# A shared expert's second products, cut into two halves of the array

## The chip, the cores and the metric

The kernel runs on one core of a Trainium2 chip. The metric is the device time of one execution in microseconds (us), as the median of several runs. All data are float32. The engines are PE (matrix products; its weight loads have a row of their own, PEld), DVE (vector), ACT (activation), POOL and SP (which issue transfers, POOL also the indirect ones).

## The reference

The reference is one block of a network: gated cross attention, then a gated mixture of experts. `x` has 4 batches of 512 tokens of 512 features.

```python
x = x + tanh(g_xattn) * xattn(layernorm(x), ctx)      # 512 x 512 attention weights from ctx
n = layernorm(x)
shared = (silu(n @ Wg_s) * (n @ Wu_s)) @ Wd_s          # 512 -> 352 -> 512, for every token
probs  = sigmoid(n @ Wr + br + rb)                     # 8 experts, the best 2 per token
routed = sum over the 2 chosen e of w_e * (silu(n @ Wg[e]) * (n @ Wu[e])) @ Wd[e]
x = x + tanh(g_ffn) * (shared + routed)
```

The change lies in the last product of `shared`, the one with `Wd_s`.

## The kernel before, in words

The kernel works in three stretches of one program; loops are unrolled when it is built, and a tile framework places the waits and the order of each engine's queue.

The first stretch, up to about 181 us, computes the attention, the normalised rows, the routing and the shared expert's hidden values. For each of 16 tiles of 128 tokens, `shared_hidden` (L464) makes the products with `Wg_s` and `Wu_s`, `pg` and `pu`, 352 columns each, and sends the hidden rows through a scratch in memory, so that they come back in a layout that DVE can turn.

The second stretch is `shared_out`, about 181 to 235 us. For tile `n`, which this document calls group `n`, `shared_turned` has DVE turn the hidden values of the next tile (the stream transposes of L331) into `hT_s`, which has two buffers, each with three chunks (`NF` = 3) of 128 hidden values by 128 tokens. `shared_back` loads the hidden rows of a tile four ahead, and `shared_down` makes the second products. It calls `down` (L568): three products, accumulated in one PSUM tile `po`, each with a chunk of `hT_s` (128 x 128) as the weights that are held in the array, and 512 columns of `wsd` (which is `Wd_s`) streaming through. Then one DVE operation (L595) adds the scaled result to the tile of `x`, and a transfer on SP's queue (L596) stores it. `po` comes from the pool `ps_out`, which has two buffers.

Between the groups PE makes a few small products for the routing tables, each asked to come after the product before it: `pw` (L642, one column of weights, 39 columns streamed) before this stretch, and `pq` and `pi` (128 columns of weights, 39 streamed) behind groups 6 and 7. DVE makes the lists of rows from them, and POOL gathers the rows of the routed blocks with indirect transfers (L750).

The third stretch, up to about 499 us, is the loop over routed blocks: 128 gathered rows of one expert each, first products `rg` and `ru` (L785, eight of 352 columns) and second products `po` (L568 again, three of 512 columns), whose weighted results are added to the output by indirect transfers (L813). The last two groups of the shared expert, 14 and 15, are issued beside the first blocks. Block 0's rows are turned by DVE behind the update of group 13 (`after(turned, done, ...)`).

PE runs each product of the code as two passes, each with its own weight load and its own instruction, so the profile counts twice as many as the code. In the profile's rows `128*128` gives the rows and columns of the weights, and `128x512` the weights' depth and the columns that stream.

Of the kernel before, what the change touches and what calls it, by code (L numbers as in the profile page):

```python
# [9 lines left out]
F32 = mybir.dt.float32  # L10
# [7 lines left out]
P = 128  # L18
# [4 lines left out]
def flamingo_block(  # L23
# [16 lines left out]
    nc = tc.nc  # L40
    B, S, D = x.shape
# [9 lines left out]
    NF = len(FT)  # L51
# [21 lines left out]
    ps_out = ctx.enter_context(tc.tile_pool(name="ps_out", bufs=2, space=PSUM))  # L73
# [64 lines left out]
    def after(later, earlier, reason="written before it is read"):  # L138
        tc.add_manual_dep(
            later.ins, earlier.ins.name,  # L140
            mybir.DependencyInfo(mybir.DependencyClass.Sync, mybir.DependencyReason.DATA),
            reason=reason,
        )
# [22 lines left out]
    hT_s = [sp.take(NF, P) for _ in range(2)]  # L166
# [26 lines left out]
    wsd = const.tile([P, NF, D], F32, tag="wsd", name="wsd")  # L193
# [131 lines left out]
    def from_quarters(by, z, engine=nc.sync):  # L325

        return engine.dma_start(out=z, in_=by.rearrange("(p b) w -> p (b w)", b=NQ))
# [7 lines left out]
    product = {}  # L335
# [228 lines left out]
    def down(hT, wdj):  # L564

        po = ps_out.tile([P, D], F32, tag="out", name="po")
        for j in range(NF):
            product["last"] = nc.tensor.matmul(  # L568
                po, lhsT=hT[:, j, :], rhs=wdj(j), start=(j == 0), stop=(j == NF - 1)
            )  # L570
        return po

    def shared_back(n, behind=None):
        if n < B * NS:
            back = from_quarters(
                hs_d[n * NQ * P : (n + 1) * NQ * P, :],
                zhs_v[n % AHEAD].rearrange("p b w -> p (b w)"), nc.scalar,
            )
            if behind is not None:
                after(back, behind, "it comes in early enough")  # L580

    def back_early(behind):
        for k in range(AHEAD):
            shared_back(k, behind)
# [5 lines left out]

    def shared_down(n):

        po = down(hT_s[n % 2], lambda j: wsd[:, j, :])
        xs = x_sb[n // NS][:, n % NS, :]
        done = nc.vector.scalar_tensor_tensor(xs, po, tgf, xs, ALU.mult, ALU.add)  # L595
        nc.sync.dma_start(out=out[n * P : (n + 1) * P, :], in_=xs)  # L596
        return done

    def shared_out(b, lo=0, hi=NS, behind=None):
        for n in range(b * NS + lo, b * NS + hi):  # L600
            if n == 0:
                shared_turned(0, behind[0])
                shared_turned(1, behind[1])
            elif n + 1 < B * NS:
                shared_turned(n + 1)
            shared_back(n + AHEAD, product.get("out"))
            done = product["out"] = shared_down(n)
        return done
# [72 lines left out]
    def count():  # L681
# [19 lines left out]
        out=tab.rearrange("b p t -> b (p t)"), in_=slot_d.rearrange("(b p) t -> b (p t)", p=P)  # L701
# [159 lines left out]
    last = SURE - 1  # L861
# [84 lines left out]
```

## Time and profile before

| what | value |
| --- | --- |
| median of 5 runs | 516.13 us (515.26 to 517.04) |
| profiled execution: its own time | 514.88 us |
| profiled execution: span from first to last instruction | 511.9 us |
| mean granted TensorE clock | 0.99 |
| PE busy | 493.6 us, 96% of the span |
| PEld, DVE, ACT, POOL busy | 275.3, 232.9, 91.4, 265.0 us |
| second products of the shared expert (L568, `po<-wsd,wqk`) | 96 passes, 42.2 us busy |
| second products of the routed blocks (L568, `po<-wbig,x_all`) | 222 passes, 101.4 us busy |
| first products of the routed blocks (L785) | 592 passes, 223.6 us busy |

How to read it: the busy time of PE counts the time in which at least one product is in the array, and a product's own duration (592 ns for 512 columns) is longer than the distance to the next one, since products follow each other through the array. The time between the starts of two products is therefore the better measure of what one costs. The span leaves out some 3 us around the program.

### The profile page before, as it was taken

Reading aid. Unit: us, or ns where it says so; the run is one execution under the profiler, and the core shown is the slowest. Engines: PE = TensorE matmul, PEld = TensorE weight load, DVE = VectorE, ACT = ScalarE, POOL = GpSimd, SP = SyncE. Lnnn points to the kernel's source line nnn. Section 1 sums busy time; section 2 is a strip of 40 time slices with the busy share of each in tenths; the row PEclk is TensorE's granted clock in tenths of the full one; section 3 lists DMA queues with packets and bytes.
Section 4 is the critical chain, followed back from the end, with each engine's and each line's share of the span. In section 5 each row is a group of like instructions: output and inputs, shape, how many; then the busy total and the mean of one; then the engine's idle time right before and its main releaser. Section 6 shows DMA issues by size and latency. Waiting matters only on the chain. (4 is left out here: it accounts for less than half of the span.)

```text
span 511.9 us, 5436 instructions
## 1 busy us (share of the span) xinstructions
PE 493.6 (96%) x1507; PEld 275.3 (54%) x1507; DVE 232.9 (46%) x542; ACT 91.4 (18%) x163; POOL 265.0 (52%) x293
## 2 busy tenths in 40 slices
PE   8999999999999999999999999999999999999980
PEld 4444464465677644455555555555555555555540
DVE  1898965855864447543323332233232233233210
ACT  3354034112023000001111111111110211111110
POOL 3004230171265510555777777777477776767331
PEclk9999999999999999999999999999999999999996
DMA  6999993579996978624556655665455665656433
GB/s 207 395 370 363 334 360 119 164 175 174 355 203 103 250 185 284 205 88 143 118 125 128 133 119 125 135 126 119 112 115 117 125 134 107 139 118 136 76 41 41
DMA packets 67164, 87.86 MB, mean 172 GB/s; under 512 B 32992, under 2 KB 40032, under 8 KB 67136
## 3 DMA queue, kind: packets, MB, share of 16 engines
q1 hardware_dynamic: 43056, 55.08, 34.9%
q0 software_dynamic: 13184, 25.88, 25.9%
q10 hardware_dynamic: 10896, 6.56, 5.2%
q8 instruction: 14, 0.23, 0.2%
q14 instruction: 14, 0.11, 0.1%
HBM read 56.78 MB, written 30.70 MB: 171 GB/s over the span
## 5 line engine op out<-in xcount | busy, mean ns | idle before, releaser
L750 POOL DMA_INDIRECT x_all<-xz_d,idx x148 | 141.4, 956 | 85.9 <-issue 35.8
L331 DVE STREAM_TRANSPOSE x_all<-x_all 128x512 f32<-128x512 f32 (+1 forms) x71 | 69.8, 984 | 156.7 <-DMA x_all<-by 141.2
L785 PE MATMUL rg<-wbig,x_all 128*128 x296 | 111.9, 460 | 1.8 <-PE po L568 1.0
L785 PE MATMUL ru<-wbig,x_all 128*128 x296 | 111.7, 459 | 0.0
L568 PE MATMUL po<-wbig,x_all 128*128 x222 | 101.4, 592 | 0.7 <-DVE x_all L836 0.7
L785 PEld LDWEIGHTS rg<-wbig,x_all 128*128 128x128 f32 x296 | 55.9, 190 | 43.3 <-issue 20.2
L813 POOL DMA_INDIRECT out_x<-ws,idx x37 | 59.6, 1611 | 29.4 <-issue 24.9
L785 PEld LDWEIGHTS ru<-wbig,x_all 128*128 128x128 f32 x296 | 56.2, 190 | 31.3
L568 PEld LDWEIGHTS po<-wbig,x_all 128*128 128x128 f32 x222 | 42.1, 190 | 44.0 <-issue 36.3
L398 PE MATMUL po<-wbig 128*128 128x512 f32 x128 | 56.4, 592 | 0.0
L464 PE MATMUL pg<-ws,wbig 128*128 128x352 f32 x128 | 49.3, 467 | 0.1
L464 PE MATMUL pu<-ws,wbig 128*128 128x360 f32 (+1 forms) x128 | 48.8, 462 | 0.0
L793 ACT ACTIVATE h_all<-rg 128x352 f32<-128x352 f32 x37 | 17.2, 464 | 173.2 <-issue 75.6
L317 POOL TENSOR_TENSOR rstd<-ve,mhalf 128x4 f32<-128x4 f32 x8 | 8.2, 1023 | 71.6 <-DVE ve L315 38.2
L812 ACT ACTIVATE ws<-po,wts 128x512 f32<-128x512 f32 x37 | 25.4, 687 | 103.1 <-PE po L568 47.5
L568 PE MATMUL po<-wsd,wqk 128*128 128x512 f32 x96 | 42.2, 594 | 0.0
L552 POOL DMA_INDIRECT slot_d<-ent,posi x32 | 31.0, 969 | 17.6 <-issue 10.1
L398 PEld LDWEIGHTS po<-wbig 128*128 128x128 f32 x128 | 24.2, 190 | 29.4 <-issue 27.5
L464 PEld LDWEIGHTS pu<-ws,wbig 128*128 128x128 f32 x128 | 24.3, 190 | 13.6
L464 PEld LDWEIGHTS pg<-ws,wbig 128*128 128x128 f32 x128 | 23.5, 190 | 12.2 <-issue 0.5
L568 PEld LDWEIGHTS po<-wsd,wqk 128*128 128x128 f32 x96 | 18.0, 190 | 21.3 <-issue 19.8
L795 DVE TENSOR_TENSOR x_all<-h_all,ru 128x352 f32<-128x352 f32 x34 | 17.5, 515 | 17.8 <-ACT h_all L793 14.0
(135 smaller groups left out, 335.0 us busy)
## 6 DMA issues: line engine op xcount, KB each, us to landing
wbig<-in_Wgu SPq DMA_DIRECT2D x8, 1408.0 KB
by<-x_all SPq DMA_DIRECT2D x34, 192.0 KB
x_all<-by SPq DMA_DIRECT2D x34, 192.0 KB
wbig<-in_Wd SPq DMA_DIRECT2D x8, 768.0 KB
x_all<-in_x SPq DMA_DIRECT2D x4, 1024.0 KB
wbig<-in_xT SPq DMA_DIRECT2D x4, 1024.0 KB
xz_d<-wbig POOLq DMA_DIRECT2D x16, 256.0 KB
wbig<-xz_d SPq DMA_DIRECT2D x16, 256.0 KB
```

The costliest lines, as they stand in the source:

```text
L317: power = nc.gpsimd.tensor_tensor(rstd, ve, mhalf, ALU.pow)
L331: return nc.vector.transpose(dst.rearrange("p c (j b) -> p b c j", b=NQ), z.rearrange("p b (c i) -> p b c i", i=Q))
L398: product["last"] = nc.tensor.matmul(po, lhsT=xT_v[b % 2][:, c, ts(s, P)], rhs=attT_v[b % 2][:, c, :], start=(c == 0), stop=(c == NN - 1),)
L464: product["last"] = nc.tensor.matmul(dst, lhsT=xnT_v[b % 2][:, c, ts(s, P)], rhs=ws[:, c, at : at + n], start=(c == 0), stop=(c == ND - 1),)
L552: sc = nc.gpsimd.indirect_dma_start(out=slot_d, in_=what, out_offset=bass.IndirectOffsetOnAxis(ap=where, axis=0), in_offset=None,)
L568: product["last"] = nc.tensor.matmul(po, lhsT=hT[:, j, :], rhs=wdj(j), start=(j == 0), stop=(j == NF - 1))
L750: g = nc.gpsimd.indirect_dma_start(out=z[:, q, :], out_offset=None, in_=xz_d, in_offset=at(idx4[:, q, i : i + 1]),)
L785: nc.tensor.matmul(dst, lhsT=xgT[:, c, :], rhs=wbig[:, bass.ds(base[i] + (c * 2 * H + lo), H)], start=(c == 0), stop=(c == ND - 1),)
L793: silu = nc.scalar.activation(sg, pg, AF.Silu)
L795: nc.vector.tensor_mul(h[:, :H], sg, pu)
L812: nc.scalar.activation(y, po, AF.Copy, scale=wts[:, i : i + 1])
L813: nc.gpsimd.indirect_dma_start(out=out, in_=y, out_offset=at(idx[:, i : i + 1]), in_offset=None, compute_op=ALU.add)
```

## The change

The second products of the shared expert are made by a new function, `down2`. It splits the 128 columns of weights (128 tokens) into two times 64. The first half is placed in columns 0 to 63 of the array and its results go to partitions 0 to 63 of `po`; the second half is placed in columns 64 to 127 and its results go to partitions 64 to 127. For each of the three chunks both halves stream the same 512 columns of `wsd`. The routed blocks keep `down`.

```diff
+    def down2(hT, wdj):
+
+        po = ps_out.tile([P, D], F32, tag="out", name="po")
+        for j in range(NF):
+            for t in range(2):
+                product["last"] = nc.tensor.matmul(
+                    po[t * 64 : (t + 1) * 64, :], lhsT=hT[:, j, t * 64 : (t + 1) * 64], rhs=wdj(j),
+                    start=(j == 0), stop=(j == NF - 1), tile_position=(0, t * 64),
+                )
+        return po
+
     def shared_back(n, behind=None):
...
     def shared_down(n):
 
-        po = down(hT_s[n % 2], lambda j: wsd[:, j, :])
+        po = down2(hT_s[n % 2], lambda j: wsd[:, j, :])
         xs = x_sb[n // NS][:, n % NS, :]
         done = nc.vector.scalar_tensor_tensor(xs, po, tgf, xs, ALU.mult, ALU.add)
```

## The prediction

> **What bounds the kernel now.** I read the page's engine shares first, then its groups, then busy time by stage, then the timeline around the lines that the change touches. Page, engines and the two groups that are replaced (count, busy us, mean ns, idle before):
>
> ```profile
> PE 493.6 (96%) x1507; PEld 275.3 (54%) x1507; DVE 232.9 (46%) x542; ACT 91.4 (18%) x163; POOL 265.0 (52%) x293
> ...
> L568 PE MATMUL po<-wsd,wqk 128*128 128x512 f32 x96 | 42.2, 594 | 0.0
> ...
> L568 PEld LDWEIGHTS po<-wsd,wqk 128*128 128x128 f32 x96 | 18.0, 190 | 21.3 <-issue 19.8
> ```
>
> PE is busy 96% of the span, and the shared expert's second products never wait (idle 0.0). The 48 products of the code stand as 96: each float32 product runs as two passes, each with its own weight load. Busy time by stage (PE, PEld, DVE, ACT, POOL; clock, DMA):
>
> ```profile
> 181.50:234.70 53.20, 52.33 (x142) 25.58 (x141) 30.73 (x52) 1.39 (x3) 17.23 (x21) 1.00 0.63 192
> 234.70:498.64 263.94, 261.38 (x790) 148.77 (x789) 81.81 (x109) 40.66 (x71) 183.10 (x167) 1.00 0.56 118
> 498.64:511.90 13.26, 1.36 (x4) 0.29 (x2) 0.00 (x0) 0.69 (x1) 1.57 (x1) 0.63 0.30 40
> ```
>
> The products lie in the first stage. The second, the routed blocks, has PE busy for 261.38 of 263.94 us at full clock. So whatever the first stage gains or loses on PE moves the end by as much. Weight loads of the first stage:
>
> ```profile
> 182.38 0.19 PEld L568 LDWEIGHTS po<-wsd,wqk 128*128 128x128 f32 x1 [0.24 <-issue]
> 182.81 0.19 PEld L568 LDWEIGHTS po<-wsd,wqk 128*128 128x128 f32 x1 [0.24 <-issue]
> ...
> 189.68 0.19 PEld L568 LDWEIGHTS po<-wsd,wqk 128*128 128x128 f32 x1 [0.24 <-issue]
> ```
>
> From 182.38 to 189.68 are 17 passes, 0.429 us each for 512 columns: that is the price of a pass. A load starts every 0.43 us, when the pass before its own starts, and is hidden under it. Loads are no limit here, so halving their width saves nothing.
>
> **The change, part by part.** It removes 48 products of 128 columns of weights (96 passes, 41.2 us) and adds 96 of 64 columns (192 passes). Each still streams 512 columns. Bytes, DMAs, DVE's, ACT's, POOL's and SP's instructions stay, in the same order. On PE the order is t=0, t=1 within each j, and 39 half products stand between the second set of small products and routed block 0 where 20 whole ones stood; 3 and 6 follow blocks 0 and 1 where 1 and 3 did.
>
> *Do the halves overlap?* No two products share the array in this trace. The bounds are 0 us extra (each pass of one half beside one of the other) and one pass of 0.429 us for each of the 96 added. The two halves write other partitions and hold other weights; nothing in the order makes the one wait for the other. I take overlap and keep the other end as a rival.
>
> *Stagger.* PE takes A-first, A-second, B-first, B-second in order (A, B the halves). A-second must wait for A-first, and B-first stands behind it. So B runs one pass late: A-second beside B-first, then B-second beside the next step's A-first. That costs one pass of 0.429 us for each uninterrupted run. The runs: groups 0 to 6; group 7; groups 8 to 13 with half of 14; the rest of 14; group 15. Before block 0 something else ends last:
>
> ```profile
> 217.64 3.17 PE L568 MATMUL po<-wsd,wqk 128*128 128x512 f32 x7
> ...
> 219.13 0.75 DVE L595 SCALAR_TENSOR_TENSOR x_all<-po,tgf,x_all 128x512 f32<-128x512 f32 x1 [1.05 <-PE po L568]
> ...
> 219.80 0.88 DVE L331 STREAM_TRANSPOSE wqk<-h_all 128x384 f32<-128x384 f32 x1
> ...
> 220.50 2.21 DVE L331 STREAM_TRANSPOSE x_all<-x_all 128x512 f32<-128x512 f32 x2
> ...
> 221.68 0.83 PE L785 MATMUL rg<-wbig,x_all 128*128 x2 [0.87 <-issue]
> ```
>
> Of the seven passes from 217.64 on, the third is group 13's last and ends streaming at 218.93 (217.64 + 3 x 0.43). DVE's update, its turn and block 0's turn then let block 0 start 2.75 us later, whatever PE does in between. So group 13's delay counts in full, the half of group 14 before block 0 is free, and the 3 half products after it need 4 passes in a row where 2 stood. One pass each for three runs, two for the fourth, one for the fifth: 6 x 0.429 = 2.6 us. Bounds 0 and 2.6; I take 2.6.
>
> *Array reshaped.* The nearest row is `pw`, one column of weights, between full ones (PE, then PEld):
>
> ```profile
> 178.21 0.76 PE L464 MATMUL pu<-ws,wbig 128*128 128x352 f32 x2
> 178.89 0.23 PE L642 MATMUL pw<-pick,eoff 128*1 128x39 f32 x2
> 179.05 0.86 PE L464 MATMUL pg<-ws,wbig 128*128 128x352 f32 x2
> ```
> ```profile
> 178.89 0.09 PEld L642 LDWEIGHTS pw<-pick,eoff 128*1 128x1 f32 x2 [0.49 <-issue]
> 179.05 0.30 PEld L464 LDWEIGHTS pg<-ws,wbig 128*128 128x128 f32 x2
> 179.45 0.19 PEld L464 LDWEIGHTS pu<-ws,wbig 128*128 128x128 f32 x1
> ```
>
> A 352-column pass takes 0.295 us (0.429 x 352 / 512). `pu`'s second starts at 178.50 and streams until 178.80, but `pw`'s load starts at 178.89: 0.09 us of drain. The two passes of `pw`, 39 columns each, need 0.07 us, until 178.96; the next load starts at 179.05: again 0.09. It is exposed: `pg`'s first pass lasts from 179.05 to 179.45, 0.10 more than its streaming. Leaving the split shape costs 0.09 + 0.10 = 0.19, entering it 0.09 + 0.056 (an exposed load of 64 columns, below) = 0.15. Five entries and four exits (the exit before block 0 lies in the idle 0.87): 5 x 0.15 + 4 x 0.19 = 1.5 us. Bounds 0 and 9 x 0.19 = 1.7.
>
> *Exposed loads.* Where products are short, loads set the pace:
>
> ```profile
> 199.55 0.86 PEld L642 LDWEIGHTS pq<-pick,ws 128*128 128x128 f32 x7 [0.24 <-issue]
> ```
>
> Seven loads in 0.86 us, the last 0.19 long: (0.86 - 0.19) / 6 = 0.112 us each for 128 columns, so I estimate 0.056 for 64. Today each load starts with the pass before its own and not earlier. If that holds, B-first's load starts when A-second starts, and B-first cannot start for 0.056 us, though its half is free; the next A-first stands behind B-second likewise. Two exposed loads a step, on the path for 46.5 steps (42 before group 14, 1.5, and 3): 93 x 0.056 = 5.2 us. Bounds: 0, if the queue pulls loads past a waiting product, and 93 x 0.112 = 10.4, if a narrow load is no faster. I take 5.2, since the row shows no load ahead of the product before it.
>
> *Added waits.* From group 2 on (and at the routed blocks 0 and 1) the first product also waits for its own engine's group two back, whose PSUM tile it takes. That group is always over by then, so it waits for nothing. The second wait puts an entry on PE's sequencer, 12 in the phase, 51 ns each by the trace. It is hidden because the sequencer reaches block 0's first entry at 218.1, 2.5 us before PE's last pass ahead of that block ends (220.65); uncovered, 12 x 0.05 = 0.6 us. DVE turns group n+1's input by 1.75 us after group n-1 ends (218.93 to 220.68 above); PE needs it after 2.57 us today, after 2.14 with the stagger: still covered.
>
> Sum: 2.6 + 1.5 + 5.2 = **9.3 us**. The profiled execution took 514.88 us (span 511.9 and 3.0 around it), so it would be 524.2. The median of the five runs, 516.13, is 1.25 above (0.24%): **525.4 us**. Runs of one kernel spread over 515.26 to 517.04, so 0.2%, 1.0 us, is about what a measurement can tell from no change.
>
> Two rules of the Trainium skill bear on this; no number here rests on them. "TensorE: Matmul & The Clock Gate", Part 3 on packing small matmuls, says that products in different tiles of the array start some 4 ns apart: by that estimate stagger and loads shrink to 96 x 0.004 = 0.4 us, and with the 1.5 the time is 518.0. Its measurements were of tiles with one product each, and no run here shows it for two passes. The same section says that a load overlaps running products only where the row groups differ; both halves use all rows, so by it every load would be exposed, 186 x 0.056 = 10.4 us, and the time 530.6. The trace contradicts it for today's loads, which lie under products of the same rows. "TensorEngine Tiling (Array Packing)", Overview, promises a factor only where a dimension is 64 or less; here it is 128, cut in two, so at best two half products cost what one did. That is a rule against a gain.
>
> **The rivals.**
> 1. *Loads pulled ahead.* As forecast, but B-first's load passes the waiting A-second: 2.6 + 1.5 = 4.1 us, 520.2. For: that half's earlier pass is over, so nothing holds its weights. Against: no load in the trace runs ahead of the product before it.
> 2. *The halves do not overlap.* 192 passes in a row. 42 steps more by 0.858 are 36.0; the half of group 14 after block 0 is 6 passes instead of 2, 1.7; group 15, 12 instead of 6, 2.6; with 1.5 for the shapes 41.8 us: **557.9**. For: all products of this trace run one behind the other, and nothing shows two at once. Against: no shared weights or partitions.
> 3. *Shorter passes, faster.* Were a pass of 64 columns of weights quicker, 96 passes on the path would gain. From rival 1's 4.1 us it breaks even at 4.1 / 96 = 0.043 us less a pass (0.386), and at half a pass (0.214) it saves 20.6 and the stagger halves to 1.3: 498.3. Against: `pw` with one column of weights and `pq` with 128 both have products of 198 ns over 39 columns; width does not set the pass.
> 4. *Nothing to measure.* Both halves start together, loads hidden and reshaping mostly covered by the drain: under 1 us, 516 to 517. With the 1.5 in full it would be 517.6, already slower.
>
> **How the numbers follow.** Forecast 0.38 (about 523 to 531), rival 1 0.27 (518 to 522), rival 2 0.25 (553 to 570, since exposed loads can add to it), in between 0.02, rival 4 0.05, rival 3 0.03. So faster 0.03, same 0.05, slower 0.92. The range goes from 518, below rival 1, to 560, above rival 2's sum. It leaves out rivals 3 and 4 and some 0.1 of rival 2's upper tail.
>
> **What would show it.** Passes of `po<-wsd,wqk` with 64 columns, 192 of them. Forecast: loads of `t`=1 start with the preceding pass and a pair of passes takes 0.485 us, the phase (181.5 to block 2's start) grows by 9. Rival 1: pairs at 0.429. Rival 2: starts 0.43 apart throughout and PE busy in the phase near 95 us. Rival 3: passes under 0.39. I am wrong in mechanism if PE idles for its own semaphore, if entering the split shape costs more than 0.2 us, or if the routed blocks change.

## The result and the profile after

The changed kernel takes 518.64 us (median of 30 runs, 516.27 to 522.89) beside 515.21 for the kernel before (56 runs, 513.27 to 520.96): a ratio of 1.0061, 95% interval 1.0044 to 1.0079, which is 3.1 us more (2.3 to 4.1). It is slower, as forecast, but by a third of the forecast 9.3 us. Here and below medians are over all runs, while ratios compare only runs in the usual state and leave out those in a slower one, with a lower granted clock, so that a ratio is not the quotient of the two medians. The profiled execution took 517.37 us, its span 515.5.

From the page, engines and the two groups that took the place of the old ones (in a group's row: count, busy us, mean ns, idle before; the lines of the code behind the new function have moved by 11):

```profile
PE 494.7 (96%) x1603; PEld 270.4 (52%) x1603; DVE 234.1 (45%) x542; ACT 91.2 (18%) x163; POOL 265.0 (51%) x293
...
L578 PE MATMUL po<-wsd,wqk 128*64 128x512 f32 x192 | 43.3, 595 | 1.9 <-DVE wqk L331 1.9
...
L578 PEld LDWEIGHTS po<-wsd,wqk 128*64 128x64 f32 x192 | 13.9, 137 | 28.5 <-issue 27.6
```

Twice the passes (192 for 96) keep PE busy for 43.3 us where it was 42.2, and a pass lasts as long as before (595 ns for 594). So two passes lie side by side nearly all the time. New is an idle 1.9 us: PE waited once for DVE's turn of a group's input. Busy time by stage (PE, PEld, DVE, ACT, POOL; clock, DMA):

```profile
180.50:237.80 57.30, 54.53 (x237) 21.31 (x236) 31.41 (x51) 1.39 (x3) 17.91 (x21) 1.00 0.58 180
237.80:502.00 264.20, 261.80 (x791) 149.01 (x790) 81.86 (x108) 40.66 (x71) 182.29 (x167) 1.00 0.55 118
502.00:515.50 13.50, 1.11 (x3) 0.19 (x1) 0.00 (x0) 0.69 (x1) 1.71 (x2) 0.67 0.28 39
```

The difference lies in the stretch of the change, 57.30 us for 53.20; the routed blocks behind it take 264.20 for 263.94. By the starts of products in the two traces: this stretch begins 0.97 us earlier than before (a difference of the unedited first stretch), block 0 starts 2.69 us later after its beginning, block 2 a further 1.44 us later after block 0, and the rest is 0.39 longer: 3.55 us, the difference of the spans. The device times of these two executions, 517.37 and 514.88 us, are only 2.49 apart, since 3.0 us lay around the span before and 1.9 lie around it now.

How the halves run shows in the loads and in the length of the uninterrupted runs on PE (start, length, engine, how many passes):

```profile
180.55 0.20 PEld L578 LDWEIGHTS po<-wsd,wqk 128*64 128x64 f32 x4 [0.49 <-issue]
181.03 0.14 PEld L578 LDWEIGHTS po<-wsd,wqk 128*64 128x64 f32 x2 [0.29 <-issue]
181.46 0.14 PEld L578 LDWEIGHTS po<-wsd,wqk 128*64 128x64 f32 x2 [0.28 <-issue]
```
```profile
180.55 18.25 PE L578 MATMUL po<-wsd,wqk 128*64 128x512 f32 x84
198.72 1.08 PE L653 MATMUL pq<-pick,ws 128*128 128x39 f32 x8
199.74 2.80 PE L578 MATMUL po<-wsd,wqk 128*64 128x512 f32 x12
202.46 0.66 PE L653 MATMUL pi<-pick,ws 128*128 128x39 f32 x4
203.06 10.52 PE L578 MATMUL po<-wsd,wqk 128*64 128x512 f32 x48
215.47 7.05 PE L578 MATMUL po<-wsd,wqk 128*64 128x512 f32 x30 [1.89 <-DVE wqk L331]
223.40 0.83 PE L796 MATMUL rg<-wbig,x_all 128*128 x2 [0.88 <-issue]
...
228.30 1.93 PE L578 MATMUL po<-wsd,wqk 128*64 128x512 f32 x6
...
237.82 0.86 PE L796 MATMUL rg<-wbig,x_all 128*128 x2
```

The same places in the kernel before:

```profile
181.52 18.19 PE L568 MATMUL po<-wsd,wqk 128*128 128x512 f32 x42
...
221.68 0.83 PE L785 MATMUL rg<-wbig,x_all 128*128 x2 [0.87 <-issue]
...
226.49 1.02 PE L568 MATMUL po<-wsd,wqk 128*128 128x512 f32 x2
...
234.66 0.76 PE L785 MATMUL rg<-wbig,x_all 128*128 x2
```

Four loads stand at the start, two for each half (each half's second load is put in behind its first pass), and from then on two loads every 0.43 us, both under the passes before. The passes start in pairs: 181.028 and 181.035, 181.458 and 181.464, 181.887 and 181.893, so 6 to 7 ns within a pair and 0.429 us from pair to pair. The 84 passes of the first run take 18.25 us; the 42 whole ones took 18.19. There is no late half and no exposed load inside a run. The row at 228.30 is the exception: group 14's rest behind block 0 is three half products, six passes, and takes 1.93 us (A is the half in columns 0 to 63, B the other). Two of B's passes start beside A's, then B's other two follow alone: four steps where the kernel before had two.

The new wait, seen on DVE (updates L606 and turns L331):

```profile
208.48 0.75 DVE L606 SCALAR_TENSOR_TENSOR x_all<-po,tgf,x_all 128x512 f32<-128x512 f32 x1 [1.04 <-PE po L578]
209.14 0.87 DVE L331 STREAM_TRANSPOSE wqk<-h_all 128x384 f32<-128x384 f32 x1
213.81 0.75 DVE L606 SCALAR_TENSOR_TENSOR x_all<-po,tgf,x_all 128x512 f32<-128x512 f32 x1 [3.79 <-PE po L578]
214.47 0.84 DVE L331 STREAM_TRANSPOSE wqk<-h_all 128x384 f32<-128x384 f32 x1
```

In groups 0 to 9, 12 and 13 the update starts 0.63 to 0.64 us after the start of the group's last pass. Group 10's last pass started at 210.41, so its update was due at 211.05; it started at 213.81, since PE's signal is recorded at 213.78, 2.8 us late, though all passes were in time. The turn for group 12 stood behind that update, and PE waited for it.

### The profile page after: what moved, and what is told of

Its sections match the earlier page's. It is cut to its first block, busy times and chain, and to the rows that moved or that the text cites. A ratio compares the mean times of both kernels' runs of the same rounds, so it can differ in the third digit from the quotient of the medians.

```text
span 515.5 us, 5641 instructions
## 1 busy us (share of the span) xinstructions
PE 494.7 (96%) x1603; PEld 270.4 (52%) x1603; DVE 234.1 (45%) x542; ACT 91.2 (18%) x163; POOL 265.0 (51%) x293
## 5 line engine op out<-in xcount | busy, mean ns | idle before, releaser
L331 DVE STREAM_TRANSPOSE x_all<-x_all 128x512 f32<-128x512 f32 (+1 forms) x71 | 70.0, 987 | 153.2 <-DMA x_all<-by 139.2
L804 ACT ACTIVATE h_all<-rg 128x352 f32<-128x352 f32 x37 | 17.2, 464 | 182.0 <-PE rg L796 83.5
L578 PE MATMUL po<-wsd,wqk 128*64 128x512 f32 x192 | 43.3, 595 | 1.9 <-DVE wqk L331 1.9
L578 PEld LDWEIGHTS po<-wsd,wqk 128*64 128x64 f32 x192 | 13.9, 137 | 28.5 <-issue 27.6
```

The source lines that it names most:

```text
L331: return nc.vector.transpose(dst.rearrange("p c (j b) -> p b c j", b=NQ), z.rearrange("p b (c i) -> p b c i", i=Q))
L578: product["last"] = nc.tensor.matmul(po[t * 64 : (t + 1) * 64, :], lhsT=hT[:, j, t * 64 : (t + 1) * 64], rhs=wdj(j), start=(j == 0), stop= ...
L804: silu = nc.scalar.activation(sg, pg, AF.Silu)
```

## The experiments

The theory after the result: (1) the two halves overlap because they are two halves of the array; (2) a half is fed past the other's waiting product, so neither stagger nor loads cost anything in a run; (3) what remains is reshaping, 0.35 us for each way in and out, and the uneven cut of group 14. The rivals: the overlap or the order comes from something else; the time is the late signal's; a reshaping costs less or more. Each kernel was timed against the kernel before on the same chip. Those chips were slower (before 522.59, 523.93 and 521.7 in the three sets), so ratios are what is compared.

**The changed kernel again**, unedited.

> The changed kernel once more, unedited. Theory (the halves run beside each other as pairs 0.429 us apart, and the loss is 1.4 us for reshaping the array plus 0.86 us because the half of group 14 is cut at an odd number of half products): some 2.2 to 3.5 us over the kernel before, and in the profile the pairs again 0.429 apart, with the 1.9 us in which PE waited for DVE gone or elsewhere. Rival (that wait is a lasting cost of the split): the same wait of about 1.9 us in the same group 12.

523.38 us (12 runs), ratio 1.0035 (1.0001 to 1.0070), or 1.8 us more: under the expected 2.2 to 3.5, which lies within the interval (0.1 to 3.7). The trace repeats the structure: 42.06 us from the first split product to block 0 (42.85 in the first profile, 40.16 before) and 19.26 from there to the first second product of the routed blocks, the same 19.26 as in the first, 17.71 before. A late signal came again, now in group 11 and 1.7 us late, and cost PE 0.9 us.

**One half's chunks first, then the other's.**

```diff
-        for j in range(NF):
-            for t in range(2):
+        for t in range(2):
+            for j in range(NF):
```

> All three products of the first half, then all three of the second. Theory (each half takes its next product from the queue on its own, past waiting products of the other half): pairs stay 0.429 us apart as long as the queue looks 12 instructions ahead, and the time is that of the changed kernel plus at most 0.9 us, since group 14 then leaves 6 passes behind block 0 instead of 4. Rival (products start strictly in the order of the program and the pairs seen are an order that was built in): the first half's six passes run alone and the second half's mostly too, about 4 passes more for each group, 16 x 4 x 0.429 = 27 us over the changed kernel.

533.11 us (4 runs), ratio 1.0192 (1.0130 to 1.0253). The start of its stretch:

```profile
187.55 0.19 PEld L578 LDWEIGHTS po<-wsd,wqk 128*64 128x64 f32 x2 [0.49 <-issue]
187.55 4.99 PE L578 MATMUL po<-wsd,wqk 128*64 128x512 f32 x20
188.03 0.14 PEld L578 LDWEIGHTS po<-wsd,wqk 128*64 128x64 f32 x1 [0.29 <-issue]
188.46 0.19 PEld L578 LDWEIGHTS po<-wsd,wqk 128*64 128x64 f32 x3 [0.29 <-issue]
188.89 0.19 PEld L578 LDWEIGHTS po<-wsd,wqk 128*64 128x64 f32 x2 [0.23 <-issue]
```

A's passes start alone at 187.548 and 188.028. B's first load starts at 188.462 and its pass at 188.463, 6 ns after A's third pass, while A's fourth to sixth were still to come. (Which half a pass belongs to is read from the distance: two of one half never start closer than 0.429 us, as the kernel with both in one half shows below.) So B does pass work that waits, but not from any depth. When A's third pass (the first of its second product) had just started, two products of A stood ahead: the one in work and one waiting whole, together five loads and passes waiting. At A's second pass there were seven, and B did not start. Each run of the stretch thus begins with two passes of A alone and ends with two of B alone (12 passes of group 7 took 3.70 us where the changed kernel took 2.80). Both simple stories, in order and unlimited, fail here.

**Two chunks of a half at a time.** This separates the two readings of that trace: a half is fed past one whole waiting product, or hardly past anything.

```diff
-        for j in range(NF):
-            for t in range(2):
+        for j, t in ((0, 0), (1, 0), (0, 1), (1, 1), (2, 0), (2, 1)):
```

> The changed kernel with the six half products of a group in another order: chunks 0 and 1 of the first half, chunks 0 and 1 of the second, then chunk 2 of the first and of the second. Where A's first pass of a run starts, five instructions wait ahead of B's first load (the product of A's second pass, loads and products of A's third and fourth). Theory (each half takes work past about five waiting instructions, not past seven): B's first load and pass start within 0.02 us of A's first pass, pairs stay 0.43 us apart, a group every 2.58 us, and the second stretch up to block 0 lasts about 42 us as in the changed kernel (41 to 43.5, a wait for DVE of up to 3 us as there aside); time within 0.3% of the changed kernel, some 1.004 of the kernel before. Rival (a half is fed past one waiting product only): B's first pass starts one or more passes late at the start of each run, 0.43 to 0.86 us for each of five runs, so 2.1 to 4.3 us more than the changed kernel, and single passes of A show at the run's start.

522.04 us (10 runs), ratio 1.0034 (0.9992 to 1.0075), that of the repeat of the changed kernel. Its first group:

```profile
186.92 0.20 PEld L577 LDWEIGHTS po<-wsd,wqk 128*64 128x64 f32 x4 [2.49 <-DVE eoff_i L705]
186.92 2.80 PE L577 MATMUL po<-wsd,wqk 128*64 128x512 f32 x12 [1.93 <-DVE eoff_i L705]
187.40 0.15 PEld L577 LDWEIGHTS po<-wsd,wqk 128*64 128x64 f32 x2 [0.28 <-issue]
```

B starts 13 ns after A (186.919, 186.932), with two products of A ahead of it, and the 12 passes take 2.80 us as in the changed kernel. By the count used above six loads and passes of A were waiting, since A's second load starts only at 186.972. The theory holds from a second side, and the rival (one or more passes late) is out. The stretch up to block 0 took 41.67 us. No signal of PE came late here; group 0's update started 0.34 us late, since DVE was still in a turn. The cut of group 14 behind block 0 is more uneven (two whole products of B, then chunk 2 of both): six steps where the changed kernel has four and the kernel before two, and the time from block 0 to the first routed second product is 20.12, 0.86 or two passes more than 19.26.

**Both halves in one half of the array.** Columns 0 to 63 and partitions 0 to 63 serve both; the sums of the two halves fall together and only 64 rows of each tile of `x` are updated.

```diff
-                    po[t * 64 : (t + 1) * 64, :], ...
-                    start=(j == 0), stop=(j == NF - 1), tile_position=(0, t * 64),
+                    po[:64, :], ...
+                    start=(j == 0 and t == 0), stop=(j == NF - 1 and t == 1), tile_position=(0, 0),
```

> Both 64-column products of each step are placed in columns 0 to 63, so that they share one half of the array; the sums of both go to the same 64 partitions, and only those 64 rows of x are updated. Theory (it is the two halves that let products run together): no overlap, 192 passes 0.429 us apart, 40 to 43 us over the kernel before, about 557. Rival (narrow products overlap or run faster wherever they stand): as the changed kernel, about 518.

561.97 us (one run), 39 us over the kernel before on that chip. The group on PE, and the same first run of 84 passes:

```profile
L578 PE MATMUL po<-wsd,wqk 128*64 128x512 f32 x192 | 83.5, 593 | 0.0
```
```profile
182.65 36.26 PE L578 MATMUL po<-wsd,wqk 128*64 128x512 f32 x84
```

Busy 83.5 us where the changed kernel has 43.3, and 36.26 us for the 84 passes that took 18.25. So the overlap comes from the two halves and from nothing else in the change, and it is worth what rival 2 had priced: by the trace 76.77 us up to block 0 and 23.54 from there to the first routed second product, 42.4 more than 40.16 and 17.71.

**The last two groups whole.** Groups 14 and 15 use `down` again; group 13's exit is then the last.

```diff
-        po = down2(hT_s[n % 2], lambda j: wsd[:, j, :])
+        po = (down2 if n < 14 else down)(hT_s[n % 2], lambda j: wsd[:, j, :])
```

> Groups 14 and 15, which stand beside the first routed blocks, keep whole products; groups 0 to 13 are split. Theory: two entries and two exits of the split shape (0.69 us by the changed kernel's trace) and the odd cut (0.86) go, 1.55 us less than the changed kernel, some 0.7 to 1.5 us over the kernel before. Rival (the loss lies in the split groups themselves, their waits or doubled instructions): no more than 0.4 us less than the changed kernel.

521.84 us (12 runs), ratio 0.9992 (0.9962 to 1.0022). From block 0 to the first routed second product it takes 17.71 us, as before to the hundredth, where the changed kernel takes 19.26:

```profile
230.24 1.02 PE L568 MATMUL po<-wsd,wqk 128*128 128x512 f32 x2
...
235.83 2.74 PE L568 MATMUL po<-wsd,wqk 128*128 128x512 f32 x6
```

So 1.55 us of the change are spent on group 14's cut and on going in and out around blocks 0 and 1. The stretch up to block 0 remains longer, 41.22 for 40.16. The ratio's interval is too wide to price the rest: it lies below that of the changed kernel in the first result, but overlaps that of the repeat on this chip (1.0001 to 1.0070), so that the saving is shown by the trace and not by the time.

**One chunk of three whole**, so that each group goes out of the split shape and back in.

```diff
         for j in range(NF):
+            if j == 1:
+                product["last"] = nc.tensor.matmul(
+                    po, lhsT=hT[:, j, :], rhs=wdj(j), start=False, stop=False
+                )
+                continue
             for t in range(2):
```

> In every group the products of j=0 and j=2 are split and that of j=1 is whole, so that the array is reshaped 16 more times in and out. Theory (each in and out costs 0.10 of drain and 0.107 of exposed load on leaving, 0.094 and 0.051 on entering, 0.35 us, as the changed kernel's trace has it): 16 x 0.35 = 5.6 us over the changed kernel, 7 to 9 over the kernel before. Rival (only the drains cost, the loads are hidden): 16 x 0.19 = 3.0, 5 to 6 over the kernel before. Rival (reshaping is free and the loss is elsewhere): as the changed kernel, 2 to 3 over.

529.34 us (12 runs), ratio 1.0084 (1.0049 to 1.0118): 4.4 us more than before. The groups on PE:

```profile
194.59 1.94 PE L583 MATMUL po<-wsd,wqk 128*64 128x512 f32 x8
196.46 1.13 PE L578 MATMUL po<-wsd,wqk 128*128 128x512 f32 x2
197.51 1.94 PE L583 MATMUL po<-wsd,wqk 128*64 128x512 f32 x8
```

From 194.59 to 197.51 are 2.92 us for a group; six passes of 0.429 are 2.57. So 0.35 us go to each way out and in, the 0.15 and 0.19 of the prediction; the groups that neither wait nor are interrupted all take this 2.92 us. The time does not confirm it: the theory expected 7 to 9 us over the kernel before, and 4.4 (2.6 to 6.2) fits the rival in which only the drains cost, 5 to 6. Against that rival stands the trace, where the loads are exposed in each group; why the timed loss is smaller is open. The signal of group 10 came 1.5 us late here. The first group's update came 2.2 us late too, but behind a turn of DVE that began only at 188.69; PE's signal had been there in time, at 187.15.

**Four quarters of 32 columns.**

```diff
-            for t in range(2):
+            for t in range(4):
-                    po[t * 64 : (t + 1) * 64, :], ...  tile_position=(0, t * 64),
+                    po[t * 32 : (t + 1) * 32, :], ...  tile_position=(0, t * 32),
```

> Four products of 32 columns each, in the four quarters of the array. Theory (every tile takes its own work from a queue that looks some six waiting instructions ahead): four passes at once; the fourth quarter's load stands behind up to nine waiting instructions and comes late, so the sets are 0.43 to 0.50 us apart and the time is 2 to 9 us over the kernel before. Rival (only two products can stream at once): 0.86 us for each set, 40 us over.

532.95 us (4 runs), ratio 1.0176 (1.0130 to 1.0221). The group on PE and the waits:

```profile
L578 PE MATMUL po<-wsd,wqk 128*32 128x512 f32 x384 | 44.6, 594 | 2.8 <-DVE x_all L606 2.2 <-DVE wqk L331 0.6
```
```profile
PE pu L464 <- DVE place L526: 4.6, 1, 4.6
PE po L578 <- DVE x_all L606: 2.2, 1, 2.2
```

Four passes start at once (191.734, .741, .747, .754) and the next four 0.429 us later, so 384 passes keep PE busy 44.6 us: the overlap holds for four tiles as for two. The expected delay of the fourth quarter did not come. Its load for the next product starts at 191.755 with nine loads and passes waiting ahead of it, three of each other quarter; so the limit that the two kernels above had shown, six waiting but not seven, is not one on their sum. A limit for each tile would fit all these kernels, but was not tested by itself. The time does not come from the passes but from waits. One is the late signal again, 4.3 us in group 10, of which PE felt 2.2. The other, 4.6 us, lies in the first stretch, which this kernel does not edit. The same wait stands in the profiles of the unedited repeat (0.9 us) and of two chunks at a time (2.9), and in neither of the first two profiles.

**Short products split.** In the kernel before, the router's products `pr` of the last two batches (8 columns streamed, limited by their loads) as two halves, and as four quarters; the second products stay whole.

```diff
-                    pr[:, s - lo, :], lhsT=xnT_v[b % 2][:, c, ts(s, P)], rhs=ws[:, c, 2 * H :],
+                for t in range(0, P, 64):          # 32 in the other kernel
+                        pr[t : t + 64, s - lo, :],
+                        lhsT=xnT_v[b % 2][:, c, s * P + t : s * P + t + 64], rhs=ws[:, c, 2 * H :],
+                        ... tile_position=(0, t),
```

> The kernel before with its shared second products whole, and the router's products of batches 2 and 3 (8 columns streamed, so that the loads set the pace: 16 passes in each of four places) split in halves. Theory (the loads of two halves run beside each other, as they started 6 ns apart in the changed kernel, each 0.056 us): 4 x 16 x 0.056 = 3.6 us saved, less four times in and out at up to 0.35: 2 to 3 us faster than the kernel before. Rival (loads take turns): no saving, 1 to 1.5 us slower.

> As e8_logits_halves with quarters of 32 columns. Theory (four loads at once, the floor being the 0.034 us between the starts of passes of 39 columns): 4 x 16 x 0.078 = 5.0 us saved less 1.4, 3 to 4 us faster than the kernel before. Rival (the number of instructions sets the pace, eight for each set at some 6 ns): 0.05 us a set, as e8_logits_halves, 2 to 3 faster. Rival (loads take turns): slower by 1 to 2.

527.75 us (9 runs), ratio 1.0060 (1.0017 to 1.0104), and 532.53 (6 runs), 1.0171 (1.0135 to 1.0207): slower, where a gain was expected. For the quarters, PE's waits between 130 and 178 us and the busy time by stage:

```profile
PE pr L444 <- issue: 5.1, 6, 1.2
PE pu L466 <- DVE place L528: 4.4, 1, 4.4
```
```profile
150.00:160.00 10.00, 5.57 (x20) 2.71 (x22) 5.60 (x16) 0.46 (x1) 3.99 (x6) 0.69 0.97 172
160.00:170.00 10.00, 4.34 (x67) 2.95 (x68) 0.17 (x1) 0.00 (x0) 5.65 (x6) 0.67 0.07 8
```

PE was busy for 4.34 of 10 us and the granted clock fell to 0.67, where the kernel before had 1.00 in every stage from 130 to 182 us. Two things ended last. DVE stood idle for 6.9 us before a turn of reloaded rows, with `place`, which PE needed, queued behind:

```profile
154.00 1.99 DVE L331 STREAM_TRANSPOSE wbig<-wbig 128x512 f32<-128x512 f32 x2 [6.90 <-issue]
155.84 0.18 DVE L528 TENSOR_TENSOR place<-pl,first 128x32 f32<-128x32 f32 x1
```

And then PE issued the short products four at a time with up to 1.2 us between, waiting for nothing that the profile shows. The first is the wait that the quarters of `po` had too (4.6 us), with that part of the code unedited, so it does not need this split. The two runs are inconclusive about what splitting a load-bound product brings. The quarters' profile shows that these many tiny products in a row were not issued at the pace of their loads.

## Why the prediction was right or wrong

| term | forecast, us | shown, us |
| --- | --- | --- |
| halves overlap | 0 extra | 0 extra (39 more without, one half) |
| stagger | 2.6 | 0.86, in one run of five |
| reshaping | 1.5 | 1.38 |
| exposed loads | 5.2 | 0 |
| added waits | 0 | 0 by themselves; 2.0 behind the late signal of the profiled run |
| sum | 9.3 | 2.24, and 3.1 (2.3 to 4.1) timed |

*The overlap* was taken rightly, and its other end, rival 2, was priced rightly: 42 us forecast, 39 timed and 42.4 by the trace in the kernel that keeps both halves in one.

*The exposed loads failed.* The step was: today each load starts with the pass before its own and not earlier, so a load will not pass a waiting product. The row showed no load ahead of its predecessor because, with one tile over the whole array, nothing else could start. It was a limit of the kernel before, read as a limit of the engine. The kernel with both halves in one half of the array shows it again: inside a run each load starts 2 ns after the pass before its own (183.131 after 183.129), so what lets a load run ahead is the other half. With two tiles, B's load and its pass start while A's second pass waits, and this costs 6 to 7 ns a pair instead of two loads of 0.056 us. The width of the loads was right: at the start of a run each half's second load starts 0.055 us after its first.

*The stagger failed in the same step*, at "A-second must wait for A-first, and B-first stands behind it". B does not stand behind A's waiting product, neither with one of A's products unfinished (the changed kernel) nor with one more waiting whole (two chunks at a time); with two more waiting it does (one half first). What is left is the cut of group 14, three half products behind block 0, where the halves are uneven: 0.858 us, two passes, as the prediction had counted for that run, only for another reason.

*The reshaping* was sized rightly: 0.70 us before block 0, 0.59 between block 0 and block 2, 0.10 for the load behind them. The 0.35 for a way out and in was then seen by itself in the trace of the kernel with one chunk whole, though its time rose by less than that sum.

*The added waits* cost nothing by themselves, but the reasoning "covered" held only while PE's signals come in time. The prediction named PE's wait for its own work as a sign of error; what came was a wait for DVE, behind a late signal. What delays it is open. It came in the profiles with several products side by side, mostly in groups 9 to 11, and more with four tiles (3.1, 4.3 and, in group 14, 4.0 us) than with two (0.3 to 2.8); with whole products, with the halves in one half of the array, and with two chunks at a time it did not come there. How much of it is in the timed runs is open too: the 2.24 us that reshaping and the uneven cut make lie just under the interval of the first result (2.3 to 4.1), and the repeat gave 1.8 (0.1 to 3.7), so neither needs more than 1.9 us of it, and the repeat needs none.

Of the rivals, "loads pulled ahead" had the right mechanism for the loads and kept the stagger: 4.1 us, just at the upper end of the interval. "Both halves start together" was given 0.05 and was the nearest in its mechanism; its full reshaping gives 517.6 us, and with the cut's 0.86 and the 1.4 instead of 1.5, 518.4 against the base of 516.13. Against rival 3 the prediction read 198 ns for the products of both `pw` and `pq`; of `pq`'s eight only the shortest takes 198, and their median is 282. That the width of the weights does not set the pass is shown by the result instead: 595 ns with 64 columns and 594 with 32, for 594 with 128.

The Trainium skill's page "TensorE: Matmul & The Clock Gate", Part 3, has both a rule that nearly held and one that did not. Products in different tiles start some 4 ns apart by it: here it was 6 to 7, and 13 with two chunks at a time, and the estimate by that rule, 518.0, was the better one; the prediction set it aside because a tile had two passes. That part also says that products start and end strictly in program order; here the measurement decides otherwise, since the kernel with one half first shows B's first pass at 188.463 ahead of A's fourth at 188.887.

## What to carry to other kernels

Cutting weights that already fill the array gains nothing: 128 columns in two halves cost the same steps, plus 0.35 us for each stretch between whole products. If products are split, keep the split ones together, cut runs where the tiles are even, and let the tiles take turns product by product, since a tile was fed past one whole waiting product of another but not past two. And a row that never shows a thing (a load ahead of a waiting product) bounds nothing where the kernel gave it no occasion.

## What was not expected of the hardware

- Two and four column tiles run fully side by side with float32's two passes each: pairs 6 to 7 ns apart, sets 0.429 us apart.
- The order of starts is not the order of the program: B passes the waiting product of A, with six loads and passes of A waiting but not with seven; with four tiles one passed nine, three of each other tile.
- PE's signal for a finished group can come late, by up to 4.3 us with four tiles, with every pass in time.
